# One LSTM step of a fused transformer kernel: both zero products side by side, the copies of the input part last on ScalarE, and the output rows reloaded step by step

## The chip, the cores and the metric

One Trainium2 chip, one core. The engines are named as the profile names them: PE (TensorE's matmuls), PEld (TensorE's weight loads), DVE (VectorE), ACT (ScalarE), POOL (GpSimd) and SP (SyncE, which issues most DMAs). The metric is device time in microseconds (us); lower is better.

## The reference, cut to what matters

A tokenizer with attention, a windowed attention layer, a mixture of experts, a phase-memory attention, and last an LSTM over T = 569 positions of 16 sequences, with D = 256 hidden units. All is fp32. What the change touches is the LSTM:

```python
x_proj = jnp.einsum('btd,gd->btg', x, W_ih) + b_ih + b_hh
def step(carry, xp):
    h, c = carry
    gates = xp + h @ W_hh.T
    i, f, g, o = jnp.split(gates, 4, axis=-1)
    c = jax.nn.sigmoid(f) * c + jax.nn.sigmoid(i) * jnp.tanh(g)
    h = jax.nn.sigmoid(o) * jnp.tanh(c)
    return ((h, c), h)
_, hs = jax.lax.scan(step, (h0, c0), jnp.swapaxes(x_proj, 0, 1))
```

After the scan, each position's output row adds a running sum over the positions before it and one over those behind it; the second needs the last position, so every output row gets one more addition at the end.

## The kernel before

Up to about 1710 us the kernel computes the tokenizer, the windowed attention and the experts. From there to about 3340 us it runs the 569 steps of the LSTM (the generator `steps()`, "the chain"), and between their instructions, up to step 505 or so, the phase-memory attention and the input products x @ W_ih of later blocks of positions ("the filler": `fronts`, `backs`). Up to the end it also runs the output sums of groups of finished steps (`all_sums`). The last 30 us add the last sum to all rows and store them.

The order on PE, DVE, ACT and POOL is fixed before the kernel runs: a planner (`class Order`) holds a table `STEP` with the cost of each part of a step, its engine and the part that it follows, and puts a piece of filler ahead of a part of the chain only where, by its own figures, it fits. SP's instructions are ordered by the compiler's tile framework. The framework also sets semaphore waits: an instruction that must wait for one semaphore carries the wait itself, and one that must wait for two gets an instruction EVENT_SEMAPHORE ahead of it on its engine, which carries the first.

One step, with the lines of the profile:

1. "hidden" (L1734): 16 matmuls of the hidden state X with W_hh, added to the PSUM tile GC (`gates`, 128x96: the gates i, f and g). "out hidden" (L1743): 8 matmuls into GO (`out_gate`, 128x64: gate o).
2. "gates" (L1754): ACT reads GC, tanh into `act`. "out gate" (L1760): ACT reads GO into `to`.
3. "clear" (L1684): four small bf16 matmuls with zeros, which set GC to zero and start its accumulation; "input" (L1691): ACT copies the next step's input part from `xc` into GC. The next "hidden" adds to it.
4. DVE: "products" `ab` (L1766), "cell" (L1772), "cell turned" `cT` (L1779).
5. "out clear" (L1684) of GO. From the last block but one on, eight spare matmuls with the identity matrix (L1085, `out_gate<-W_hh,ident`) stand ahead of it; they write to GO what the clear then overwrites.
6. "tangent" (L1787): ACT, tanh of the cell into `th`. Then "out input" (L1696): ACT copies `xo` into GO.
7. DVE: "out gate turned" (L1792), "state" X (L1794). X is what the next "hidden" waits for.

Each unit of 8 steps has its input part loaded by SP (one DMA `xc`, L1675, and four `xo`, L1679). Rows that are finished while filler runs are stored to a DRAM tile PD, since there is no room for them in SBUF. When the filler ends its SBUF is released, a tile O for all output rows takes its place, and SP reloads PD into O with eight DMAs of up to 1 MB (L1905). Later rows are written to O directly (L1863).

Of the kernel before, what the change touches and what calls it, by code (L numbers as in the profile page):

```python
# [10 lines left out]
F32 = mybir.dt.float32  # L11
BF16 = mybir.dt.bfloat16
AF = mybir.ActivationFunctionType
# [4 lines left out]
D = 256  # L18
# [67 lines left out]
def time_of_rows():  # L86
# [43 lines left out]
    "hidden": ("PE", 0.68, 0.85, "state", 0.055),  # L130
    "out hidden": ("PE", 0.24, 0.42, "hidden", -0.17),
    "gates": ("ACT", 0.16, 0.26, "hidden", 0.065),
    "clear": ("PE", 0.06, 0.25, "gates", 0.06),
    "out gate": ("ACT", 0.12, 0.22, "out hidden", 0.065),
    "input": ("ACT", 0.14, 0.24, "clear", 0.065),
    "products": ("DVE+", 0.22, 0.22, "gates", 0.035),
    "cell": ("DVE+", 0.19, 0.19, "products", 0.035),
    "cell turned": ("DVE", 0.13, 0.21, "cell", 0.035),
    "out clear": ("PE", 0.06, 0.25, "out gate", 0.06),
    "tangent": ("ACT", 0.14, 0.23, "cell turned", 0.095),  # L140
    "out input": ("ACT", 0.12, 0.22, "out clear", 0.065),
    "out gate turned": ("DVE", 0.15, 0.23, "out gate", 0.035),
    "state": ("DVE+", 0.18, 0.18, "tangent", 0.035),
}
# [150 lines left out]
def kernel(ctx: ExitStack, tc: tile.TileContext, a: dict, out: bass.AP):  # L295
    nc = tc.nc
# [1367 lines left out]
    def steps():  # L1664

        act = ls.tile([128, 4 * 32], F32, name="act_init", tag="act", bufs=3)
        nc.vector.memset(act[:, 96:], 0.0)
        before, begun, loaded = None, set(), set()  # L1670

        def load(k):
            j, u, n = UNITS_ALL[k]
            loaded.add(k)
            nc.sync.dma_start(  # L1675
                XC[k % 2][:, :n, :], XCD[j][:, :, u : u + n, :].rearrange("a b t x -> (a b) t x")
            )
            for q in range(4):
                nc.sync.dma_start(XO[k % 2][32 * q + NB : 32 * q + 32, :n, :], XOD[j][q, :, u : u + n, :])  # L1679
            plan.mark(("loaded", k), 4.0)  # L1680

        def clear(g, n, last):
            for q in range(4):
                nc.tensor.matmul(  # L1684
                    g[32 * q : 32 * q + 32, :n], nil[:, :32], nil[:, :n], start=True, stop=last
                )

        def begin(k, t):
            begun.add((k, t))
            yield "input"  # L1690
            nc.scalar.copy(GC[:, :96], XC[k % 2][:, t, :])  # L1691

        def begin_out(k, t):
            begun.add((k, t, "out"))
            yield "out input"
            nc.scalar.copy(GO[:, :64], XO[k % 2][:, t, :])  # L1696

        def ready(k):

            n = 2 * UNITS_ALL[k][0]  # L1700
            return [("back", n + i, slot) for i in range(2) for slot in range(2)]

        for k, (j, u, n) in enumerate(UNITS_ALL):
            if k not in loaded:
                for event in ready(k):
                    yield "at", event
                load(k)
            yield "at", ("loaded", k)

            after = [("back", 2 * (j + 1) + i, slot) for i in range(2) for slot in range(2)]  # L1710
            done = sum(plan.past(e) for e in after) if j + 1 < len(BLOCKS) else 4
            ahead = plan.past(("back", 2 * j + 3, 0))
            plan.spare = 0.0 if ahead else 0.2 if done >= 4.0 * u / BLOCKS[j][1] - AHEAD else 0.45
            if (j, u) in run_of:
                r = run_of[j, u]
                if r >= 4:
                    yield "at", ("sums", r - 4)
                hidden[r] = XS_OF[r % 4][:, :, : RUNS[r][2], :]
            X = hidden[r][:, :, u - RUNS[r][1] :, :]
            for t in range(n):  # L1720
                at, last = f"{k}_{t}", (k, t) == (len(UNITS_ALL) - 1, n - 1)
                if before is None:
                    yield "hidden"
                    clear(GC, 96, True)
                    clear(GO, 64, True)
                if (k, t) not in begun:
                    yield from begin(k, t)
                    yield from begin_out(k, t)
                yield "hidden"
                for kk in range(2 if before is not None else 0):  # L1730
                    for half in range(2):
                        for q in range(4):
                            own = 512 * (q // 2) + 96 * (2 * (q % 2) + half)
                            nc.tensor.matmul(  # L1734
                                GC[32 * q : 32 * q + NB * (1 + half), :96],
                                before[:, kk, NB * (1 - half) :], Whh[:, kk, own : own + 96],
                                start=False, stop=(kk + half == 2),
                            )
                yield "out hidden"
                for kk in range(2 if before is not None else 0):  # L1740
                    for q in range(4):
                        own = 512 * (q // 2) + 384 + 64 * (q % 2)
                        nc.tensor.matmul(  # L1743
                            GO[32 * q : 32 * q + 32, :64], before[:, kk, :],
                            Whh[:, kk, own : own + 64], start=False, stop=(kk == 1),
                        )
                if (
                    k + 1 < len(UNITS_ALL) and k + 1 not in loaded
                    and all(plan.past(e) for e in ready(k + 1))
                ):  # L1750
                    load(k + 1)
                nxt = (k, t + 1) if t + 1 < n else (k + 1, 0)
                yield "gates"
                nc.scalar.activation(act[:, :96], GC[:, :96], AF.Tanh, scale=0.5)  # L1754
                if not last:
                    yield "clear"
                    clear(GC, 96, False)
                to = ls.tile([128, 64], F32, name=f"to{at}", tag="to", bufs=3)
                yield "out gate"
                nc.scalar.activation(to, GO[:, :64], AF.Tanh, scale=0.5)  # L1760
                ahead = nxt[0] in loaded and plan.past(("loaded", nxt[0]))
                if ahead:
                    yield from begin(*nxt)
                ab = ls.tile([128, 2, 32], F32, name=f"ab{at}", tag="ab", bufs=2)
                yield "products"
                nc.vector.scalar_tensor_tensor(  # L1766
                    ab, act[:, :64].rearrange("p (g x) -> p g x", g=2), 1.0,
                    act[:, 64:].rearrange("p (g x) -> p g x", g=2), ALU.add, ALU.mult,
                )
                act = ls.tile([128, 4 * 32], F32, name=f"act{at}", tag="act", bufs=3)  # L1770
                yield "cell"
                nc.vector.scalar_tensor_tensor(  # L1772
                    act[:, 96:], ab[:, 1, :], 0.5, ab[:, 0, :], ALU.mult, ALU.add
                )


                cT = ls.tile([128, 2 * NB], F32, name=f"cT{at}", tag="cT", bufs=2)
                yield "cell turned"
                nc.vector.transpose(cT, act[:, 96:])  # L1779
                if not last:  # L1780
                    yield "out clear"
                    if j >= len(BLOCKS) - 2:
                        product(GO[:, :D], ident, Whh[:, 0, :D], start=True, stop=True)
                    clear(GO, 64, False)
                th = ls.tile([128, 2, NB], F32, name=f"th{at}", tag="th", bufs=2)
                yield "tangent"
                nc.scalar.activation(th.rearrange("p k x -> p (k x)"), cT, AF.Tanh, scale=0.5)  # L1787
                if ahead:
                    yield from begin_out(*nxt)
                toT = ls.tile([128, 2, 2 * NB], F32, name=f"toT{at}", tag="toT", bufs=2)  # L1790
                yield "out gate turned"
                nc.vector.transpose(toT.rearrange("p k x -> p (k x)"), to)  # L1792
                yield "state"
                nc.vector.scalar_tensor_tensor(  # L1794
                    X[:, :, t, NB:], toT[:, :, NB:], 1.0, th, ALU.add, ALU.mult
                )
                before = X[:, :, t, :]
            if u + n == RUNS[r][1] + RUNS[r][2]:
                plan.mark(("steps", r))

# [85 lines left out]
    with tc.manual_schedule(engines=ENGINES):  # L1886
# [13 lines left out]
        bg.close()  # L1900
        op = ctx.enter_context(tc.tile_pool(name="out", bufs=1))
        tail["O"] = op.tile([128, sum(map(len, UNITS_OF)), D], F32, name="O")
        for u in range(0, tail["stored"], 8):
            u1 = min(u + 8, tail["stored"])
            nc.sync.dma_start(tail["O"][:, u:u1, :], PD[:, u:u1, :])  # L1905
        plan.run([chain, rest])
    route.release()


# [153 lines left out]
```

## Time and profile before

| | |
|---|---|
| median of 3 runs | 3372.89 us (3368.87 to 3373.28) |
| the profiled execution | 3372.32 us, of which the span of its instructions is 3370.5 us |
| PE / DVE / ACT / POOL busy | 91% / 60% / 44% / 23% of the span |
| step 33 to step 481 (448 steps) | 1863.7 to 3092.0 us, 2.74 us per step |
| steps 514 to 569, without filler | 3192.7 to 3328.4 us, nearly all 2.50 us |
| end of the last step to the end | 3330 to 3370.5 us |

The table of waits tells for each engine and line how long it waited for whom, how often and how long at most. The chain in order of time follows back from the last instruction what released each instruction; "issue" in it is time in which nothing that the profile shows was waited for, such as the way of a semaphore from one engine to the next. ACTq is ACT's sequencer: there it is the EVENT_SEMAPHORE ahead of an ACT instruction.

### The profile page before, as it was taken

How to read it: one execution, taken by the hardware profiler on the slowest of the kernel's cores; microseconds unless marked ns; L12 is line 12 of the kernel's file. 1: busy time of each engine (PE TensorE's matmuls, PEld its weight loads, DVE VectorE, ACT ScalarE, POOL GpSimd, SP SyncE). 2: the span in 40 equal slices, each digit the busy share in tenths (PEclk: the TensorE clock that was granted, in tenths of full speed). 3: DMA queues.
4: the chain of work that ended last, by engine and by line, in shares of the span. 5: the costliest groups of instructions: out<-in, count | busy, mean ns of one | idle time of the engine just before them, and what ended most of it. 6: DMA issues, size and time to landing. Idle time of an engine off the chain costs nothing.

```text
span 3370.5 us, 135926 instructions
## 1 busy us (share of the span) xinstructions
PE 3069.8 (91%) x57536; PEld 2227.7 (66%) x57536; DVE 2013.5 (60%) x6785; ACT 1482.6 (44%) x5032; POOL 789.8 (23%) x1524
## 2 busy tenths in 40 slices
PE   6999989999859999997899999999999999999884
PEld 3666666666648888886565666666766666666552
DVE  4677777766732222222565777777777777776555
ACT  3545544454412222221443555555555555554442
POOL 1243554445533323222311011011111000100000
PEclk8999999999979999998999999999999999999997
DMA  5111221111176666663333333333333333333413
GB/s 179 53 41 62 89 79 51 55 39 40 42 254 231 224 224 228 226 234 130 110 95 78 94 82 80 86 90 87 87 82 90 91 83 84 81 91 79 144 36 117
DMA packets 272628, 366.39 MB, mean 109 GB/s; under 512 B 144097, under 2 KB 219793, under 8 KB 258961
## 3 DMA queue, kind: packets, MB, share of 16 engines
q1 hardware_dynamic: 250368, 308.51, 30.9%
q0 software_dynamic: 14496, 39.75, 3.1%
q8 instruction: 451, 7.39, 0.9%
q10 hardware_dynamic: 7152, 9.43, 0.9%
q14 instruction: 161, 1.31, 0.1%
HBM read 239.07 MB, written 118.49 MB: 106 GB/s over the span
## 4 chain that ended last, share of the span: by engine, by line
PE 40%; DVE 5%; ACT 3%; DMA 2%; issue 2%; POOL 0%; SPq 0%; ACTq 0%; DVEq 0%
PE gates L1734 12%; PE xm_False L1085 7%; PE out_gate L1743 3%; PE po_False L1085 2%; PE ek L1085 2%; PE v L1085 2%; PE eq L1085 2%; PE z L1085 2%; PE r_False L1085 1%; PE ds_False L1085 1%; PE out_gate L1684 1%; ACT act L1754 1%; PE gates L1684 1%; PE fin L1085 1%; DVE ab L1766 1%
## 5 line engine op out<-in xcount | busy, mean ns | idle before, releaser
L1734 PE MATMUL gates<-W_hh,X 128*16 128x96 f32 (+1 forms) x18176 | 487.7, 247 | 48.2 <-DVE X L1794 41.5
L1734 PEld LDWEIGHTS gates<-W_hh,X 128*16 128x16 f32 (+1 forms) x18176 | 377.5, 103 | 225.1 <-DVE X L1794 194.7
L1754 ACT ACTIVATE act<-gates 128x96 f32<-128x96 f32 x568 | 141.7, 249 | 462.9 <-PE gates L1734 453.8
L1248 ACT ACTIVATE hT<-hp,w 128x256 f32<-128x256 f32 x316 | 132.3, 471 | 481.2 <-PE hp L1241 314.1
L1766 DVE SCALAR_TENSOR_TENSOR ab<-act 128x64 f32<-128x64 f32 x568 | 127.8, 225 | 301.4 <-ACT act L1754 294.8
L1085 PE MATMUL xm_False<-W_ih,dxT_False 128*32 128x256 f32 x4352 | 294.3, 382 | 3.0 <-DVE xp_False L1591 1.2
L1255 PE MATMUL y<-w,hT 128*128 128x256 f32 x1264 | 289.7, 382 | 5.2 <-ACT hT L1248 1.5
L1241 PE MATMUL hp<-xt,w 128*128 128x256 f32 x1264 | 287.9, 381 | 1.0 <-ACT hT L1248 1.0
L1684 PEld LDWEIGHTS <-nil 128*32 128x32 bf16 x4552 | 176.4, 94 | 148.9 <-issue 55.9
L1255 PEld LDWEIGHTS y<-w,hT 128*128 128x128 f32 x1264 | 236.9, 190 | 45.1 <-ACT hT L1248 14.4
L1241 PEld LDWEIGHTS hp<-xt,w 128*128 128x128 f32 x1264 | 240.3, 191 | 35.7 <-ACT hT L1248 1.4
L1184 POOL DMA_INDIRECT YT<-ys,to x158 | 153.3, 970 | 439.9 <-DVE ys L1261 408.3
L1261 DVE TENSOR_TENSOR ys<-y,w 128x512 f32<-128x512 f32 x79 | 54.6, 691 | 316.6 <-PE y L1255 229.8
L1743 PE MATMUL out_gate<-W_hh,X 128*32 128x64 f32 x9088 | 233.8, 219 | 4.1 <-ACT out_gate L1696 2.6
L1691 ACT COPY gates<-xc 128x96 f32<-128x96 f32 x569 | 138.4, 243 | 176.9 <-PE gates L1684 104.9
L1743 PEld LDWEIGHTS out_gate<-W_hh,X 128*32 128x32 f32 x9088 | 186.9, 110 | 7.7 <-ACT out_gate L1696 2.9
L693 PE MATMUL wqk<-wxT,wqkv 128*128 128x128 f32 x1152 | 152.9, 281 | 8.6 <-ACT wxT L687 8.4
L908 POOL DMA_INDIRECT XS<-XN,at x144 | 148.9, 1034 | 45.6 <-issue 24.6
L693 PEld LDWEIGHTS wqk<-wxT,wqkv 128*128 128x128 f32 x1152 | 141.7, 194 | 25.3 <-ACT wxT L687 13.4
L1794 DVE SCALAR_TENSOR_TENSOR X<-toT,th 128x32 f32<-128x32 f32 x569 | 107.5, 189 | 77.7 <-ACT th L1787 72.4
L1298 POOL TENSOR_SCALAR r_False_rstd<-r_False_mv,cols 128x2 f32<-128x2 f32 x36 | 15.7, 436 | 584.4 <-DVE r_False_mv L1293 584.3
L1684 PE MATMUL gates<-nil 128*32 128x96 bf16 x2276 | 131.1, 209 | 23.7 <-ACT act L1754 18.5
(356 smaller groups left out, 6509.7 us busy)
## 6 DMA issues: line engine op xcount, KB each, us to landing
w<-in_wpack SPq DMA_DIRECT2D x79, 1154.0 KB
taps<-in_taps SPq DMA_DIRECT2D x16, 1764.0 KB
xc<-XCD SPq DMA_DIRECT2D x71, 384.0 KB
XCD<-xp_False SPq DMA_DIRECT2D x256, 96.0 KB
xs<-XS SPq DMA_DIRECT2D x79, 258.0 KB
yg<-YT SPq DMA_DIRECT2D x72, 256.0 KB
HD<-h SPq DMA_DIRECT2D x72, 128.0 KB
fh<-HD SPq DMA_DIRECT2D x72, 128.0 KB
```

What stands on the lines that cost most here:

```text
L693: nc.tensor.matmul(qk[:, j, m, :], wqkv[:, k, D * j + 128 * m : D * j + 128 * m + 128], xT[:, k, :], start=(k == 0), stop=(k == 1),)
L908: fill(0, nc.gpsimd.indirect_dma_start(out=XS[0], out_offset=bass.IndirectOffsetOnAxis(ap=at[:, i, c - lo : c - lo + 1], axis=0), in_=XN[p ...
L1085: nc.tensor.matmul(out[own], lhsT[:, own], rhs, start=start, stop=stop)
L1184: keep(nc.gpsimd.indirect_dma_start(out=YT, out_offset=bass.IndirectOffsetOnAxis(ap=to[:, i : i + 1], axis=0), in_=ys[:, i, :], in_offset= ...
L1241: nc.tensor.matmul(hp[:, i, :], w1[:, k, hc * 128 : (hc + 1) * 128], xT[:, k, :], start=(k == 0), stop=(k == 1),)
L1255: nc.tensor.matmul(y[:, i, :], hT[:, hc, 128 * i : 128 * i + 128], w2[:, hc, :], start=(hc == 0), stop=(hc == 3),)
L1684: nc.tensor.matmul(g[32 * q : 32 * q + 32, :n], nil[:, :32], nil[:, :n], start=True, stop=last)
L1691: nc.scalar.copy(GC[:, :96], XC[k % 2][:, t, :])
L1734: nc.tensor.matmul(GC[32 * q : 32 * q + NB * (1 + half), :96], before[:, kk, NB * (1 - half) :], Whh[:, kk, own : own + 96], start=False, ...
L1743: nc.tensor.matmul(GO[32 * q : 32 * q + 32, :64], before[:, kk, :], Whh[:, kk, own : own + 64], start=False, stop=(kk == 1),)
L1754: nc.scalar.activation(act[:, :96], GC[:, :96], AF.Tanh, scale=0.5)
L1766: nc.vector.scalar_tensor_tensor(ab, act[:, :64].rearrange("p (g x) -> p g x", g=2), 1.0, act[:, 64:].rearrange("p (g x) -> p g x", g=2), ...
```

## The change

- The two clears of a step stand side by side, after "out gate", with the spare matmuls ahead of both.
- "input" and "out input" come last in the step on ACT, after "tangent" (in the code, `begin` now holds both copies).
- The framework is told that ACT's reads of GC and GO (L1754, L1760) and ACT's copies into them need no semaphore between each other, because a PE product stands between them.
- The planner's table `STEP` gets the new order and new costs.
- PD is reloaded by pieces of two rows, one DMA per step at the end of the step, issued on ACT.

Cut to its core:

```diff
-    "clear": ("PE", 0.06, 0.25, "gates", 0.06),
     "out gate": ("ACT", 0.12, 0.22, "out hidden", 0.065),
-    "input": ("ACT", 0.14, 0.24, "clear", 0.065),
+    "clear": ("PE", 0.11, 0.3, "out gate", 0.06),
...
-    "out clear": ("PE", 0.06, 0.25, "out gate", 0.06),
-    "tangent": ("ACT", 0.14, 0.23, "cell turned", 0.095),
-    "out input": ("ACT", 0.12, 0.22, "out clear", 0.065),
+    "tangent": ("ACT", 0.18, 0.23, "cell turned", 0.04),
+    "input": ("ACT", 0.18, 0.24, "clear", 0.065),
+    "out input": ("ACT", 0.16, 0.22, "clear", 0.065),
...
+            begun[k, t] = nc.scalar.copy(GC[:, :96], XC[k % 2][:, t, :])
+            ordered_by_products(begun[k, t], read.pop(0, None))
             yield "out input"
-            nc.scalar.copy(GO[:, :64], XO[k % 2][:, t, :])
+            begun[k, t, 1] = nc.scalar.copy(GO[:, :64], XO[k % 2][:, t, :])
+            ordered_by_products(begun[k, t, 1], read.pop(1, None))
+
+        def ordered_by_products(ins, other):
+            if other is not None and before is not None:
+                tc.declare_no_dep(
+                    ins.ins, other.ins, reason="a product between them waits for the first"
+                )
+            return ins
...
                 yield "gates"
-                nc.scalar.activation(act[:, :96], GC[:, :96], AF.Tanh, scale=0.5)
+                read[0] = ordered_by_products(
+                    nc.scalar.activation(act[:, :96], GC[:, :96], AF.Tanh, scale=0.5), begun.pop((k, t))
+                )
+                to = ls.tile([128, 64], F32, name=f"to{at}", tag="to", bufs=3)
+                yield "out gate"
+                read[1] = ordered_by_products(
+                    nc.scalar.activation(to, GO[:, :64], AF.Tanh, scale=0.5), begun.pop((k, t, 1))
+                )
                 if not last:
                     yield "clear"
+                    if j >= len(BLOCKS) - 2:
+                        product(GO[:, :D], ident, Whh[:, 0, :D], start=True, stop=True)
                     clear(GC, 96, False)
-                to = ls.tile([128, 64], F32, name=f"to{at}", tag="to", bufs=3)
-                yield "out gate"
-                nc.scalar.activation(to, GO[:, :64], AF.Tanh, scale=0.5)
-                ahead = nxt[0] in loaded and plan.past(("loaded", nxt[0]))
-                if ahead:
-                    yield from begin(*nxt)
+                    clear(GO, 64, False)
...
                 yield "cell turned"
                 nc.vector.transpose(cT, act[:, 96:])
-                if not last:
-                    yield "out clear"
-                    if j >= len(BLOCKS) - 2:
-                        product(GO[:, :D], ident, Whh[:, 0, :D], start=True, stop=True)
-                    clear(GO, 64, False)
                 th = ls.tile([128, 2, NB], F32, name=f"th{at}", tag="th", bufs=2)
                 yield "tangent"
                 nc.scalar.activation(th.rearrange("p k x -> p (k x)"), cT, AF.Tanh, scale=0.5)
-                if ahead:
-                    yield from begin_out(*nxt)
+                if nxt[0] in loaded and plan.past(("loaded", nxt[0])):
+                    yield from begin(*nxt)
...
                 before = X[:, :, t, :]
+                if tail.get("reload"):
+                    part = tail["reload"].pop(0)
+                    nc.scalar.dma_start(tail["O"][:, part, :], PD[:, part, :])
...
-        for u in range(0, tail["stored"], 8):
-            u1 = min(u + 8, tail["stored"])
-            nc.sync.dma_start(tail["O"][:, u:u1, :], PD[:, u:u1, :])
+        tail["reload"] = [slice(u, min(u + 2, tail["stored"])) for u in range(0, tail["stored"], 2)]
         plan.run([chain, rest])
```

More of the change, by code (lines that the diff above doesn't have):

```diff
@@ L1669, in steps @@
         nc.vector.memset(act[:, 96:], 0.0)
-        before, begun, loaded = None, set(), set()
+        before, begun, loaded, read = None, {}, set(), {}
         def load(k):
@@ L1688, in begin @@
         def begin(k, t):
-            begun.add((k, t))
             yield "input"
-            nc.scalar.copy(GC[:, :96], XC[k % 2][:, t, :])
-        def begin_out(k, t):
-            begun.add((k, t, "out"))
+            begun[k, t] = nc.scalar.copy(GC[:, :96], XC[k % 2][:, t, :])
+            ordered_by_products(begun[k, t], read.pop(0, None))
             yield "out input"
-            nc.scalar.copy(GO[:, :64], XO[k % 2][:, t, :])
+            begun[k, t, 1] = nc.scalar.copy(GO[:, :64], XO[k % 2][:, t, :])
[6 more added lines that the diff above has]
+            return ins
         def ready(k):
@@ L1727, in steps @@
                     yield from begin(k, t)
-                    yield from begin_out(k, t)
                 yield "hidden"
@@ L1902 @@
         tail["O"] = op.tile([128, sum(map(len, UNITS_OF)), D], F32, name="O")
-        for u in range(0, tail["stored"], 8):
-            u1 = min(u + 8, tail["stored"])
-            nc.sync.dma_start(tail["O"][:, u:u1, :], PD[:, u:u1, :])
+        tail["reload"] = [slice(u, min(u + 2, tail["stored"])) for u in range(0, tail["stored"], 2)]
         plan.run([chain, rest])
+        assert not tail["reload"]
     route.release()
```

## The prediction

> **What bounds the kernel now.** First the table of stretches: busy time of PE, PEld, DVE, ACT and POOL, then the granted clock, DMA share and GB/s.
>
> ```profile
> 2600.00:2800.00 200.00, 193.96 (x5938) 136.73 (x5942) 150.39 (x575) 111.44 (x444) 19.26 (x48) 1.00 0.36 91
> 3188.00:3338.00 150.00, 117.08 (x3688) 78.84 (x3680) 79.08 (x341) 64.26 (x285) 0.00 (x0) 0.98 0.09 24
> ```
>
> With filler PE is 97% busy, without it 78%. But a busy PE does not say who is late. The table of waits does:
>
> ```profile
> PEld gates L1734 <- DVE X L1794: 194.7, 428, 1.0
> ```
>
> In 428 of 568 steps the first weight load of "hidden" finds nothing ahead of it and waits for X, 0.45 us on average. PE's matmuls are still draining then, so PE looks busy, but the step's length is set by the chain X, hidden, gates, cell, tangent, X. A microsecond on that chain counts 428 times, with filler or without. One step of it, from the chain in order of time:
>
> ```profile
> 3240.61 0.02 issue
> 3240.63 0.02 ACTq L1754
> 3240.65 0.04 issue
> 3240.69 0.26 ACT act L1754
> ...
> 3241.68 0.02 issue
> 3241.70 0.24 ACT th L1787
> 3241.94 0.02 issue
> 3241.97 0.20 DVE X L1794
> 3242.17 0.04 issue
> 3242.21 0.90 PE gates L1734 x32
> ```
>
> Each hop costs 0.02 to 0.04 us, save the one from PE to `act`, 0.08 us: there an EVENT_SEMAPHORE (ACTq) takes the first of two waits. The copies into PSUM and PE's work ahead of them are in the timeline (start, length):
>
> ```profile
> 3241.19 0.64 PE L1085 MATMUL out_gate<-W_hh,ident 128*32 128x256 f32 x8
> 3241.32 0.24 ACT L1691 COPY gates<-xc 128x96 f32<-128x96 f32 x1 [0.18 <-PE gates L1684]
> 3241.99 0.22 ACT L1696 COPY out_gate<-xo 128x64 f32<-128x64 f32 x1
> ```
>
> Both end well ahead of "hidden" or beside it: no row of the chain is a copy.
>
> **The change part by part.** The program's order shows where the waits go. ACT's EVENT_SEMAPHOREs fall from 2671 to 1038, but PE's rise from 371 to 927. `act`, `to` and the copies now wait for PE alone. But ACT had learnt from those waits how far its own work was, and PE had learnt from X that the copy into GC was done, since X came behind `th` and `th` behind the copy. Both lose that: `th` now waits for DVE and ACT (565 of 569 steps), the first matmul of "hidden" for DVE and ACT (560 of 568), with DVE's wait in the EVENT_SEMAPHORE ahead of them. So two double waits come onto the chain and one leaves it.
>
> `act`: 0.08 us becomes 0.02: −0.06 us a step.
>
> `th`: the nearest row with both waits is the exponential in the tokenizer, which waits for DVE and ACT:
>
> ```profile
> 853.39 0.62 DVE L585 TENSOR_REDUCE ttop<-tsc 128x1 f32<-128x441 f32 x1 [0.86 <-PE tsc L579]
> 854.11 0.63 ACT L589 ACTIVATE tP<-tsc,ttop 128x441 f32<-128x441 f32 x1 [1.82 <-DVE ttop L585]
> ```
>
> The reduction ends at 854.01, the exponential starts 0.10 us later; `th` starts 0.03 us behind `cT` now. That is +0.06 to +0.07, so `act` and `th` cancel.
>
> "hidden": nearest is a matmul of the filler that waits for DVE and PE, with DVE last:
>
> ```profile
> 2740.79 0.44 DVE kT L1271
> 2741.23 0.14 issue
> 2741.36 0.64 PE r_False L1085 x8
> ```
>
> 0.14 us where "hidden" has 0.04: +0.10. Its weight load stands 0.03 us ahead of it (2741.33), so counted by weight loads it is +0.06. I take 0.085: the matmul is what "hidden" ends by. Ends 0.06 and 0.10.
>
> The copy as the later of the two: it can start when `th` leaves ACT; `to` starts 0.02 us before `act` ends, so from 3241.91, and ends at 3242.15, X at 3242.16. The clear of GC now stands behind the spare matmuls, where the clear of GO ended at 3241.86 and its copy started 0.13 us later; by that the copy ends at 3242.23. With 0.05 us to PE it is ready by 3242.20 to 3242.28; X with its double wait lets "hidden" start at 3242.30. So X stays last, by 0.02 to 0.10 us.
>
> Sum for the chain: 428 x 0.085 = +36 us (26 to 43). In the other 140 steps the wait lies under PE's queue, and I cost it at nothing; if it showed there too it would be 12 more.
>
> The planner's order: the same 493,792 columns of filler end in the same step, but less evenly. Between steps 33 and 480, steps with fewer than 512 columns rise from 13 to 29, and those with 1152 or more from 48 to 58. A piece of 256 columns takes 0.43 us (1.31 us for three, `xm_False` L1085 in the chain). Sixteen more light steps that leave one piece open are 7 us, two pieces 14; nothing if the heavy steps have room. I take +10 (0 to 15). The clears cost nothing more: they are the same instructions, under PE's queue.
>
> The reload: the chain of waits shows it where the filler ends.
>
> ```profile
> 3161.95 10.97 DMA O<-PD
> 3172.94 12.46 DMA xo<-XOD
> ```
>
> SP issued eight reloads between the first and the second of a unit's four `xo` loads, and the next input part came late. But the chain went on beside it: `act` of step 505 starts at 3158.99, of step 514 at 3190.24; nine steps took 31.25 us against 9 x 2.50 and 0.3 for the sums in them. So the whole stall is 8.4 us, not 23. Cut into 30 pieces of 256 KB behind no `xo`, I take all of it: −8.4. Nearest rows for issuing on ACT: DMAs there take ACT's sequencer 0.41 us in the experts, up to 1.57 us in the last stores; ACT has 0.8 us between "out input" and `act`. At 0.41 it is hidden; at the upper end it would be 30 x 0.75 = 22 us, which I count to a quarter in the range (+5).
>
> A rule speaks against the part of this that rests on another queue. The Trainium skill ("DMA: Bandwidth & Descriptors", "Issuing engines are not separate DMA queues") says that DMAs issued by different engines run on the same 16 DMA engines and interleave, and that a second issuer saves only issue time. By it the gain would be the cutting's alone, at worst nothing, and the sum 8.4 us higher.
>
> What comes new at that place: the first write to O must wait until the last stores out of the released SBUF have landed. Before, the last addition ended at 3156.64 and the write to O (L1863) started at 3161.01, 4.4 us later, two steps on, off the path. In the new order this write stands on DVE directly behind the last addition and ahead of the next `ab`. The addition ends 0.7 us after X, so `ab` gets DVE at 0.7 + 4.4 + 0.8 (two writes) = 5.9 us after X instead of 1.3: +4.5 us once (0 to 4.5). The first reload on ACT waits for the same landing, beside it.
>
> Against the profiled execution's own 3372.3 us (its median stands 0.6 above that): 3372.3 + 36 + 10 − 8.4 + 4.5 = 3414.4.
>
> **The rivals.** *Faster*: a second wait that is already met might cost nothing, on `th` and on "hidden"; then only `act`'s −0.06 stays: −0.06 x 428 = −26, with the reload −8, about 3338. It decides if the rise of `th` behind `cT` and of "hidden" behind X stays under 0.02 us each. Against it: `r_False`'s other wait was long met and still 0.14 us passed.
>
> *No change*: PE is 97% busy, so the filler may take up the chain's delay; then only the 56 steps from 3188 us on pay, 56 x 0.085 = 5, which with −8.4 and +4.5 gives 3373. Against it: 428 waits of 0.45 us.
>
> *Copy last*: if filler ahead of the clears, or ACT's work, lets the copy end over 0.09 us after X, the copy sets "hidden". 0.1 us more in the 428 steps is +43: about 3457. For it: the margin is 0.02 to 0.10 us, and the clears now lie behind all filler that came between the two before.
>
> **How the numbers follow.** Forecast 0.75, copy last 0.12, faster 0.08, no change 0.05. Low end: 26 + 0 − 8.4 + 0 = +18, 3390. High end: 43 + 15 + 0 (the rule) + 4.5 + 5 = +67, 3440; what is left out is the copy last, the faster case and the even one. One measurement tells about 0.2% (6.7 us) from no change. Faster by more 0.07, within 0.05, slower 0.88.
>
> **What would show it.** In the chain after: `th` about 0.09 us behind `cT`, "hidden" 0.11 to 0.14 behind X, an ACTq row no longer ahead of `act` but ahead of `th`, a PEq row or a longer issue ahead of "hidden", and steps of 2.58 us instead of 2.50 where no filler is. No DMA row of over 3 us near the filler's end, and one step of some 7 us there. I am wrong if steps without filler stay at 2.50 us or fall, if the copies L1691 and L1696 come into the chain, or if waits for X become rarer with filler.

## The result, and the profile after

The changed kernel takes 3475.6 us (median of 4 runs, 3469.4 to 3480.2) against 3372.3: 1.0311 times as long (95% interval 1.0298 to 1.0324), +103 us. The direction was right, the size was not: +42 was forecast, and the time lies 36 us above the range. The profiled execution took 3469.4 us, its span 3467.6 us.

One step behind the filler, from the chain of waits of the kernel after (start, length, what):

```profile
3301.81 0.22 DVE cT L1786
3302.03 0.02 issue
3302.05 0.02 ACTq L1789
3302.07 0.04 issue
3302.11 0.23 ACT th L1789
3302.34 0.18 ACT gates L1689
3302.52 0.15 ACTq L1802
3302.67 0.00 ACT out_gate L1692
3302.68 0.21 issue
3302.89 0.89 PE gates L1737 x32
3303.77 0.02 issue
3303.80 0.26 ACT act L1758
```

As the prediction had it, the ACTq row has left `act` and stands ahead of `th`, and "hidden" starts late: 560 of its 568 steps have an EVENT_SEMAPHORE of 0.05 us ahead of the first weight load (PEldq is the sequencer of PE), which the kernel before has nowhere at this line:

```profile
L1737 PEldq EVENT_SEMAPHORE  x560: 51/51/51, 1715.0 to 3422.9; - x187
```

But the chain runs over the two copies (L1689, L1692) and not over X. The table of waits says the same (engine, line, what it waited for: us in all, times, longest):

```profile
ACT th L1789 <- DVE cT L1786: 284.7, 479, 5.0
PEld gates L1737 <- ACT out_gate L1692: 251.9, 462, 4.9
ACT gates L1689 <- DMA xc<-XCD: 68.0, 7, 17.1
```

The prediction had said that copies in the chain would prove it wrong. Whether "hidden" really waits for a copy has to be decided by experiment, because `out_gate` L1692 is a name that the profile infers from which event came last, and by the program "hidden" does not wait for that copy at all (its matmuls write GC, not GO). The timeline has the four candidates, start and length:

```profile
3302.28 0.24 ACT L1689 COPY gates<-xc 128x96 f32<-128x96 f32 x1
3302.38 0.19 DVE L1796 SCALAR_TENSOR_TENSOR X<-toT,th 128x32 f32<-128x32 f32 x1 [0.23 <-ACT th L1789]
3302.46 0.21 ACT L1692 COPY out_gate<-xo 128x64 f32<-128x64 f32 x1
3302.68 0.51 PEld L1737 LDWEIGHTS gates<-W_hh,X 128*16 128x16 f32 x16 [0.57 <-ACT out_gate L1692]
```

The copy into GC ends at 3302.52, X at 3302.57, the copy into GO at 3302.67, the first weight load follows at 3302.68. Beside filler the copy into GC is seldom last either: of the 441 steps from 33 to 480 that do not end a block of 64, it ends after X in 20, and what it ends later than 0.06 us after X comes to 3.5 us in all.

Two other rows matter. PE stands still where the profile shows nothing to wait for, here in the middle of "out hidden" (8 matmuls in the program, 16 rows in the profile; chain of the kernel after):

```profile
2452.59 0.19 PE out_gate L1746 x10
2452.78 1.45 issue
2454.24 0.26 PE out_gate L1746 x3
```

And the seven waits for the input part of the next block have grown. In the kernel before they read:

```profile
ACT gates L1691 <- DMA xc<-XCD: 55.0, 7, 13.0
```

Laid out by stretches (from one `act` to the next, both traces): steps 33 to 480, where filler lies between the steps, take 1228.3 us before and 1316.0 after. Seven of these steps stand at the end of a block of 64 (steps 96, 160 and so on to 480); the chain there waits until the filler has made the next block's input. They took 70.0 us together and take 105.7: +36. The other 441 steps took 1158.3 and take 1210.3: +52. The first 32 steps are 6 us longer, the last 54 5 us longer, steps 481 to 514, where the reload was, 2.4 us shorter.

The granted clock, the share of its full clock that PE had by the profile, differs a little too. Between steps 33 and 480 PE ran at half its clock for 3.4 us in the trace before and for 27.3 us in the trace after, in six pieces; PE had been busy for at most 2.5 of the 4 us ahead of each. If every microsecond at half the clock costs half of one, that is 12 us more than before (an estimate, and an upper one); no run separates it from the rest of the 88 us.

### The profile page after: what moved, and what is told of

It is laid out like the page before. It is cut to its first block, busy times and chain, and to the rows that moved or that the text cites. A ratio compares the mean times of both kernels' runs of the same rounds, so it can differ in the third digit from the quotient of the medians.

```text
span 3467.6 us, 134874 instructions
## 1 busy us (share of the span) xinstructions
PE 3066.9 (88%) x57536; PEld 2272.3 (66%) x57536; DVE 2039.6 (59%) x6809; ACT 1430.0 (41%) x5008; POOL 785.8 (23%) x1524
## 4 chain that ended last, share of the span: by engine, by line
PE 29%; DVE 9%; ACT 9%; issue 4%; DMA 2%; SPq 1%; POOL 0%; ACTq 0%; DVEq 0%
PE gates L1737 12%; PE xm_False L1084 4%; ACT act L1758 2%; ACT th L1789 2%; DVE ab L1773 2%; DVE cT L1786 2%; DVE act L1779 2%; PE out_gate L1746 2%; PE ek L1084 1%; ACT gates L1689 1%; ACT out_gate L1692 1%; PE eq L1084 1%; PE po_False L1084 1%; PE v L1084 1%; PE z L1084 1%
## 5 line engine op out<-in xcount | busy, mean ns | idle before, releaser
L1737 PE MATMUL gates<-W_hh,X 128*16 128x96 f32 (+1 forms) x18176 | 501.0, 249 | 118.1 <-ACT out_gate L1692 89.3
L1737 PEld LDWEIGHTS gates<-W_hh,X 128*16 128x16 f32 (+1 forms) x18176 | 398.3, 103 | 282.9 <-ACT out_gate L1692 251.9
L1746 PE MATMUL out_gate<-W_hh,X 128*32 128x64 f32 x9088 | 254.0, 221 | 12.4 <-issue 10.9
L1789 ACT ACTIVATE th<-cT 128x32 f32<-128x32 f32 x569 | 130.3, 229 | 288.2 <-DVE cT L1786 284.7
L1746 PEld LDWEIGHTS out_gate<-W_hh,X 128*32 128x32 f32 x9088 | 202.3, 111 | 18.4 <-issue 16.0
L1689 ACT COPY gates<-xc 128x96 f32<-128x96 f32 x569 | 133.9, 235 | 88.0 <-DMA xc<-XCD 68.0
L1084 PEld LDWEIGHTS xm_False<-W_ih,dxT_False 128*32 128x32 f32 x4352 | 128.3, 110 | 51.4 <-DVE xp_False L1590 7.4
```

The source lines that it names most:

```text
L1084: nc.tensor.matmul(out[own], lhsT[:, own], rhs, start=start, stop=stop)
L1689: begun[k, t] = nc.scalar.copy(GC[:, :96], XC[k % 2][:, t, :])
L1737: nc.tensor.matmul(GC[32 * q : 32 * q + NB * (1 + half), :96], before[:, kk, NB * (1 - half) :], Whh[:, kk, own : own + 96], start=False, ...
L1746: nc.tensor.matmul(GO[32 * q : 32 * q + 32, :64], before[:, kk, :], Whh[:, kk, own : own + 64], start=False, stop=(kk == 1),)
```

## The experiments

**The theories.** A: "hidden" now has two waits; the second costs 0.09 us a step on the chain and leaves PE short of instructions. O: the rest is the order in which the planner lays the filler. The rivals: it is the zero products standing together (B); second waits cost nothing (C); the reload only moves its stall (D); the copies, which the table of waits names, set the start of "hidden" (E); the gaps of PE follow the chain's length (F); PE is so full of filler that a shorter chain gains nothing (P).

Where the experiments ran, the kernel before takes 3380 to 3386 us instead of 3372, so ratios to it are compared; the kernel after was not run again there, and where a distance to it is given in us it is the difference of the two ratios. One row for each; "gaps" are stretches over 0.3 us between steps 33 and 480 in which PE neither multiplies nor loads weights and waits for nothing that the trace shows; the last two columns are the seven block-boundary steps and the 441 others, in us. Steps and distances (end of X to the first matmul of "hidden", end of `cT` to `th`) are medians over the last 52 steps, where no filler is.

| kernel | ratio to before (95%) | step | X to hidden | cT to th | gaps: us | boundaries | others |
|---|---|---|---|---|---|---|---|
| before | 1 | 2.500 | 0.054 | 0.034 | 7: 4.5 | 70.0 | 1158.3 |
| after | 1.0311 (1.0298 to 1.0324) | 2.586 | 0.145 | 0.094 | 23: 18.3 | 105.7 | 1210.3 |
| e1 copy behind tangent | 1.0239 (1.0208 to 1.0270) | 2.584 | 0.145 | 0.034 | 23: 22.5 | 75.8 | 1228.3 |
| e2 no self-waits | 0.9982 (0.9966 to 0.9998) | 2.501 | 0.054 | 0.094 | 6: 4.1 | 65.1 | 1153.9 |
| e3 rows by steps | 0.9988 (0.9975 to 1.0000) | 2.500 | 0.054 | 0.034 | 4: 3.9 | 68.2 | 1163.7 |
| e4 zero product ahead | 1.0152 (1.0116 to 1.0187) | 2.501 | 0.054 | 0.093 | 8: 4.3 | 108.6 | 1176.0 |
| e5 one planner number | 1.0076 (1.0059 to 1.0093) | 2.500 | 0.056 | 0.034 | 7: 5.6 | 99.8 | 1157.9 |
| e6 zero products together | 1.0141 (1.0124 to 1.0158) | 2.956 | 0.056 | 0.492 | 7: 3.6 | 76.0 | 1175.3 |
| e7 planner told | 1.0135 (1.0118 to 1.0152) | 2.586 | 0.146 | 0.094 | 24: 20.2 | 36.7 | 1237.7 |
| e8 kept parts, other order | 0.9928 (0.9912 to 0.9945) | 2.500 | 0.054 | 0.095 | 7: 3.9 | 48.4 | 1171.0 |
| e9 both causes removed | 1.0041 (1.0027 to 1.0055) | 2.500 | 0.054 | 0.095 | 7: 5.8 | 69.1 | 1170.4 |
| e10 tangent freed | 0.9878 (0.9862 to 0.9895) | 2.445 | 0.055 | 0.034 | 6: 2.5 | 47.1 | 1158.5 |
| e11 hidden alone with two | 1.0260 (1.0243 to 1.0277) | 2.527 | 0.146 | 0.034 | 29: 21.4 | 105.5 | 1198.7 |

**e1: the copy into GC behind the tangent, alone.**

```diff
-                if ahead:
-                    yield from begin(*nxt)          # ahead of "products"
...
                 if ahead:
+                    yield from begin(*nxt)          # behind "tangent"
                     yield from begin_out(*nxt)
```

> The kernel before with one edit: the copy of the input part into GC stands behind the tangent on ACT instead of ahead of the products; zero products, waits of ACT on itself and reload as before. So only the first matmul of 'hidden' gets a second wait (DVE in an EVENT_SEMAPHORE, then ACT, in 561 of 568 steps); 'act' and 'th' keep their waits.
> Theory A (the second wait of 'hidden' is the cost on the chain, and its EVENT_SEMAPHORE also leaves PE short of instructions): steps without filler rise by 0.09 to 0.10 us to 2.59-2.60, gaps of PE over 0.3 us that nothing explains rise from 7 to 15 or more between steps 32 and 480, the sum of the steps that are no block boundary rises by 40 to 60 us; total 3410 to 3435.
> Rival B (the zero products together are the cost, through the order in which filler is laid): 3370 to 3385, steps of 2.50 us.
> The seven steps at block boundaries depend on the order that the planner makes of it; 60 to 90 us together.

Measured: 1.0239, 3464.7 us, above the 3410 to 3435 of theory A. This edit alone costs some 80 us. The distance to "hidden" rises by 0.091 us and nothing else in the chain moves, so a step is 2.584 us; the gaps of PE triple. The other steps rise by 70 us, of which 441 x 0.084 = 37 are the chain's and 18 the gaps'; some 15 were not taken apart (the filler lies in another order here, and PE ran at half its clock for 17.1 us instead of 3.4). Against the 40 to 60 us expected for these steps that is too much as well.

**e2: no waits of ACT on itself, alone.** The declarations of the change between copies and reads are put into the kernel before, and nothing else.

> The kernel before with one edit: the declarations that take ACT's waits on itself away between copies and reads. 'act' waits for PE alone, 'th' gets DVE and ACT; 'hidden' keeps its one wait, and the order of the filler stays the same to the instruction.
> Theory A: -0.06 us on 'act' and +0.07 on 'th' cancel: steps without filler 2.50 to 2.52 us, boundaries 70 us as before, unexplained gaps of PE as few as before; total 3365 to 3380.
> Rival C (a second wait that is met costs nothing on ACT): steps of 2.44 us, total 3340 to 3350.

Measured: 0.9982. In its chain `act` follows "hidden" without ACTq, and `th` has it instead:

```profile
3287.33 0.22 DVE cT L1790
3287.55 0.02 issue
3287.57 0.02 ACTq L1798
3287.59 0.04 issue
3287.63 0.24 ACT th L1798
```

The step stays at 2.50 us: what `act` gains `th` loses, as forecast. "Hidden" keeps its one wait. So its second wait in the kernel after does not come from ACT's missing waits on itself but, with e1, from the copy's place.

**e3: output rows by steps, alone.** The reload of the change in the kernel before.

> The kernel before with one edit: the output rows are reloaded two units at a time behind the steps, from ACT.
> Theory A (the reload's stall of 8.4 us goes, the write to O costs up to 4.5 us once): steps 504 to 514 fall from 33.7 to about 30 us with one step of some 7 us among them; all before that as it was; total 3363 to 3369.
> Rival D (the reload only moves its stall to other steps or to the end): 3370 to 3377.

Measured: 0.9988, -4.1 us (interval -8.5 to 0). Steps 505 to 514 fall from 33.7 to 26.4 us; one step of 4.9 us, not of 7, stands at the filler's end. The total fits theory A at its small end but does not separate it from D, nor from no change; the steps do. The small stall of 4.9 us is step 504, just ahead of the ten.

**e4: the kernel after with one zero product of one column ahead of "hidden".**

```diff
                 yield "hidden"
+                if before is not None:
+                    nc.tensor.matmul(GC[:32, :1], nil[:, :32], nil[:, :1], start=False, stop=False)
```

> The kernel after with one addition: ahead of 'hidden' stands one zero product of one column into GC. It takes the wait for the copy into GC (ACT), so that the first matmul of 'hidden' waits for DVE alone and PE's EVENT_SEMAPHOREs fall from 926 to 366; the order of the filler, the copies and all else stay the same to the instruction.
> Theory A: 'hidden' stands 0.04 to 0.05 us behind X instead of 0.11, steps without filler fall by 0.06 to 0.09 us to 2.50-2.52, unexplained gaps of PE fall from 23 back to under 12, and the boundaries stay at 100 to 108 us, since the order is the same; total 3415 to 3440.
> Rival E (the copies, now last on ACT, set the start of 'hidden', as the table of waits names them): nothing gained, 3470 to 3480.
> Rival B (order alone): 3465 to 3480.

Measured: 1.0152, 3438.6 us; 1.6% or 54 us (give or take 13) below the kernel after. From its timeline (the zero product is PE L1734):

```profile
3280.20 0.24 ACT L1689 COPY gates<-xc 128x96 f32<-128x96 f32 x1
3280.30 0.19 DVE L1798 SCALAR_TENSOR_TENSOR X<-toT,th 128x32 f32<-128x32 f32 x1 [0.23 <-ACT th L1791]
3280.38 0.21 ACT L1692 COPY out_gate<-xo 128x64 f32<-128x64 f32 x1
3280.50 0.16 PE L1734 MATMUL gates<-nil 128*32 128x1 bf16 x1 [0.32 <-ACT gates L1689]
3280.55 0.45 PEld L1739 LDWEIGHTS gates<-W_hh,X 128*16 128x16 f32 x22 [0.48 <-DVE X L1798]
```

The copies stand to X as in the kernel after, to within 0.01 us: the copy into GC ends at 3280.44, X at 3280.49, the copy into GO at 3280.59. But "hidden" starts at 3280.55, before the copy into GO ends. The copies did not set its start; rival E falls, and with it the name in the table of waits. What cost 0.09 us was that one instruction had two waits and the late one, X, stood in the EVENT_SEMAPHORE. The zero product takes the early wait, and X is the only one left. The gaps of PE fall back to 8 with it. The table of waits, PE alone, first of this kernel and then of the kernel after:

```profile
PE out_gate L1748 <- issue: 2.2, 4, 0.7
```

```profile
PE out_gate L1746 <- issue: 10.9, 16, 1.9
```

The boundaries stay at 108.6 us, as the unchanged order of the filler asks.

e4 also measures the order of the kernel after. It has that order with the step and the gaps of the kernel before, and still takes 1.52% or 51 us longer than it; in its trace 39 us of that are boundaries. The reload's gain (e3) and the added matmuls are in this figure, and so is a clock that stood at half for 47.8 us in this trace, that of the slowest of its four runs.

**e5: the kernel before with one number of the planner changed.**

```diff
-    "hidden": ("PE", 0.68, 0.85, "state", 0.055),
+    "hidden": ("PE", 0.68, 0.85, "state", 0.085),
```

> The kernel before with one number of the planner's table changed: it counts 0.085 us instead of 0.055 from X to 'hidden'. No instruction is added, removed or given another wait for its own sake; only the order in which filler is laid between the steps changes.
> Theory O (the sums of the block-boundary steps come from where the planner lays the filler): the seven boundaries rise from 65-70 us to 90-110, as in the kernel after; steps without filler stay at 2.50, unexplained gaps of PE under 10; the other steps fall by up to 15 us, since the filler is spread thinner there; total 10 to 30 us above before (3395 to 3415).
> Rival (the boundaries rose in the kernel after because its chain was slower): boundaries 65 to 72, total 3378 to 3392.

Measured: 1.0076, +26 us, with the chain at 2.50 us and no more gaps than before. The boundaries rise from 70 to 99.8 us by the order of filler alone; theory O. That the other steps fall by up to 15 us was not seen (1157.9).

**e6: both zero products together, alone**, behind "out gate" in the kernel before, with the copies where they were.

> The kernel before with one edit: both zero products stand together behind 'out gate', as in the kernel after; the copies stay where they were (GC ahead of the tangent, GO behind it), waits and reload too.
> Theory A: the zero product of GC now lies behind the spare product and behind filler, so the copy into GC ends later, and the tangent stands behind that copy on ACT. At the end, where the spare product takes 0.64 us of PE, steps rise from 2.50 to 2.8-3.0 us (54 steps: +16 to +27 us); between steps 32 and 480 by 0.02 to 0.06 us each. 'hidden' keeps its one wait. Total 3415 to 3450. Then the copies had to be put behind the tangent for the zero products to stand together.
> Rival (the same instructions in another place cost nothing): 3380 to 3395.

Measured: 1.0141. Its chain at the end:

```profile
3291.26 0.23 ACT to L1756
3291.49 0.04 issue
3291.53 0.64 PE out_gate L1084 x8
3292.17 0.04 PE gates L1683 x4
3292.21 0.09 PE out_gate L1683 x4
3292.31 0.02 issue
3292.33 0.07 ACT gates L1690
3292.40 0.10 issue
3292.50 0.23 ACT th L1784
```

DVE's row `cT` is gone from the chain: the tangent waits on ACT behind the copy, the copy for the zero products, these for the spare product of 0.64 us, and that for `to`. Steps become 2.96 us. So with the spare product ahead of both zero products, as the change has it, the copies have to go behind the tangent, and that costs the second wait on "hidden" (e1). The zero product of GC ahead of the spare product was not tried.

**e7: the kernel after, its planner told of the two waits.**

```diff
-    "hidden": ("PE", 0.68, 0.85, "state", 0.055),
+    "hidden": ("PE", 0.68, 0.85, "state", 0.14),
...
-    "tangent": ("ACT", 0.18, 0.23, "cell turned", 0.04),
+    "tangent": ("ACT", 0.18, 0.23, "cell turned", 0.1),
```

> The kernel after with two numbers of the planner's table changed to what its profile shows: 0.14 us from X to 'hidden' (0.055), 0.10 from the turned cell to the tangent (0.04). Every instruction keeps its waits; only the order of the filler changes.
> Theory O: the boundaries fall from 106 us to 35-70, part of it comes back in the other steps (+10 to +25), the steps without filler stay at 2.585 and the unexplained gaps of PE at 15 to 25; total 3430 to 3460.
> Rival (boundaries follow the slower chain): boundaries 100 to 110, total 3468 to 3485.

Measured: 1.0135, 1.8% or 59 us below the kernel after, by the order of filler alone: the step is still 2.586 us, the gaps are 24. The boundaries fall to 36.7 us; the waits for the input part say so too:

```profile
ACT gates L1689 <- DMA xc<-XCD: 26.0, 4, 15.9
```

27 us of the 69 come back in the other steps, a little more than the 10 to 25 expected. The total is a little under the 3430 to 3460 expected.

**e8: what is worth keeping.** The kernel before with the edits of e2 and e3, and the planner's number from X to "hidden" at 0.145.

> The kernel before with two parts of the change (ACT's waits on itself away; output rows reloaded by steps) and the planner's number from X to 'hidden' at 0.145 us. Zero products and copies as before, so 'hidden' has one wait.
> Theory A with O: steps without filler 2.50, stall of the reload gone (-5 to -7 us between steps 504 and 514), -6 for the self-waits as measured alone, boundaries 45 to 60 us instead of 65 to 70, other steps up by 0 to 8; total 3355 to 3378, below the kernel before.
> Rival (the planner's number was best where it was): boundaries 70 or more, total 3375 to 3400.

Measured: 0.9928, 3356.3 us, as theory A with O had it; the boundaries fall to 48.4 us, but the other steps rise by 13 us where 0 to 8 was expected.

**e9: the kernel after with the zero product of e4 and that number at 0.145.**

> The kernel after with the zero product of one column ahead of 'hidden' (so that 'hidden' waits for DVE alone) and the planner's number from X to 'hidden' at 0.145 us instead of 0.055 (so that filler is laid in another order). Nothing else is changed.
> Theory A with O (the two waits of 'hidden' and the filler's order are the whole of the loss): steps without filler 2.50, unexplained gaps of PE under 10, boundaries 60 to 75 us, no stall of the reload; total 3365 to 3395, within 0.5% of the kernel before.
> Rival (a third cause costs 20 us or more): above 3400.

Measured: 1.0041, 3391.3 us: 2.70 of the 3.11% are gone, which is 91 of 105 us here. Taken singly the two edits of e4 and e7 were worth 54 and 59, 22 more than that. But e9 has not the table of e7 (which also changes the tangent's number), so its order is another, with boundaries of 69.1 us instead of 36.7; whether the two causes overlap no run tells. What is left, 0.4%, was not taken apart; the first 32 steps (156.4 us against 148.6) hold about half of it.

**e10: `th` freed as well.** In the kernel of e8 the copy into GC keeps its wait for `act`:

```diff
             begun[k, t] = nc.scalar.copy(GC[:, :96], XC[k % 2][:, t, :])
-            ordered_by_products(begun[k, t], read.pop(0, None))
```

> The kernel of two kept parts in another order of filler (step behind the tangent and 'hidden' as before), with one more edit: the copy into GC keeps its wait for 'act' on ACT, 0.6 us ahead of X and off the chain. ACT learns by it how far its own work is, so 'th' waits for DVE alone while 'act' still waits for PE alone.
> Theory A: 'th' stands 0.03 us behind 'cT' instead of 0.09, steps without filler fall to 2.44 us, the steps at the end by 3 us in all, those that wait for X between steps 32 and 480 by 0.06 each where PE is not full; total 10 to 26 us below the 3356 of that kernel: 3330 to 3347.
> Rival P (PE full of filler takes it up): 3350 to 3362.

Measured: 0.9878, 3340.6 us: 40 us below the kernel before and the fastest version. No ACTq is left in its chain:

```profile
3182.47 0.26 ACT act L1761
3182.73 0.02 issue
...
3183.24 0.22 DVE cT L1789
3183.47 0.02 issue
3183.49 0.24 ACT th L1797
3183.73 0.02 issue
3183.75 0.20 DVE X L1804
3183.95 0.04 issue
3184.00 0.90 PE gates L1740 x32
```

**e11: the kernel after with the edit of e10**, so that "hidden" alone has two waits.

> The kernel after with one edit: the copy into GC keeps its wait for 'act' on ACT. So 'act' and 'th' have one wait each, 'hidden' keeps two, and the order of the filler stays the same to the instruction.
> Theory A (the gaps of PE follow the EVENT_SEMAPHORE ahead of 'hidden'): steps without filler 2.52 to 2.53, unexplained gaps still 18 to 28, boundaries 100 to 110; total 15 to 27 us below the kernel after, 2.3 to 2.8% above before.
> Rival F (the gaps follow the longer chain): with the step a third as far above 2.50 as in the kernel after, gaps of about 12 or fewer, and a total under 2.2% above before.

Measured: 1.0260, 17 us below the kernel after. The step falls to 2.527 us, the gaps do not fall with it (29). They follow the EVENT_SEMAPHORE ahead of "hidden", not the length of the chain: 23 to 29 in the four kernels that have it, 4 to 8 in the nine that have not. Where no filler is, another thing sets the step here. With `th` earlier, X ends 0.07 us ahead of the copy into GC, which waits for the zero products and the spare product, and the chain runs over that copy:

```profile
3291.09 0.25 ACT gates L1689
3291.35 0.07 issue
3291.41 0.89 PE gates L1736 x32
```

"Hidden" starts as far behind X as in the kernel after (0.146), and its weight load 0.05 behind the copy, so the two waits end together here. Between steps 33 and 480 X is the last in most steps (by 0.085 us, median), as in the kernel after.

## Why the prediction was wrong

In short, two terms of the sum failed: the planner's order, taken at +10 us, was worth some 51, and the second wait of "hidden", taken at +36, some 54.

**The bound.** Right: X, "hidden", gates, cell, tangent set the step; e4 and e10 take 0.085 and 0.055 us off it against the kernel that they alter, and gain 1.6 and 0.5%, although most steps lie beside filler.

**The chain's terms.** Right in size. `th` +0.060 (0.06 to 0.07 said), "hidden" +0.091 for the matmul and +0.062 for its weight load (0.085 taken), from the first matmul of "hidden" to `act` -0.07 (-0.06), the step +0.086 (0.085). The copy ends 0.05 us ahead of X (0.02 to 0.10 said), so the rival "copy last" did not happen, though the time lies near its 3457 and beyond, and though the profile's names spoke for it: e4 shows it without filler, and beside filler the late copies add up to 3.5 us.

**What the chain's term lacked.** 428 x 0.085 = 36 stood for the whole cost of the second wait. e4 takes that wait away in an unchanged order and gains 54 us (41 to 67). The surplus has its clearest part in the gaps of PE: 18.3 us against 4.5 in the trace. No step of the prediction asked what else an EVENT_SEMAPHORE on PE holds up. Of the other 140 steps, costed at nothing, some paid as well: in the kernel after the weight load of "hidden" waits 462 times instead of 428, for 252 us instead of 195.

**The planner's order.** This is the step that failed most: +10 us, 0 to 15, where e4 leaves 51 us (39 to 63) for the order and the smaller parts together. The seven boundaries alone are 36 us longer, e5 shows that order alone moves them by 30 without any instruction changed, and e7 takes 59 us off the kernel after by order alone. The prediction counted how many steps get few or many columns of filler. That misses where the pieces stand on which the next block's input hangs: where these come late in a block, the chain waits at its end in one go. The row with the seven waits for XC, 55 us in all, was in the table of waits of the kernel before; it should have been the basis of this term, and its range: e4, e5, e7 and the kernel after lie between 37 and 109 us.

**The reload.** The stall went, no DMA of over 3 us is left in the chain near the filler's end, and e3 measures -7.3 us in those steps (-8.4 said), -4.1 in all. Whether the other queue or the cutting brought it no run separates, so the rule of the Trainium skill ("DMA: Bandwidth & Descriptors", "Issuing engines are not separate DMA queues"), that another issuer saves only issue time, is neither shown nor refuted here. The issue on ACT took 0.33 us (0.41 taken), beside other work. The write to O made one step of 7.57 us in the kernel after, 5.0 above the others (+4.5 said), and of 4.9 in e3, 2.4 above.

**The rivals.** "Faster" and "no change" fell as argued: a second wait costs 0.06 us on ACT and 0.09 on PE (e2, e1), and the filler did not take it up (e4 gains more than the chain's share).

## What to carry to other kernels

Where a planner lays filler around a chain, a changed step table is a change of its own: price it at the places where the chain waits for the filler (here seven, 37 to 109 us in all), give it both signs, and separate it on the chip by a version that changes the table and nothing else. Before moving an instruction behind the one by which another engine learnt of it, count the waits of the first instruction that needs both; if it gets two, let a small instruction ahead of it take the one that is met first. And where only the name that the profile gives to a wait speaks for a cause, change the form of the wait and leave the named instruction where it is.

## What the runs showed of the hardware

A second wait is not free, even where it is met before the other; in the rows measured here the later of the two stands in the EVENT_SEMAPHORE: 0.060 us on ACT (e2), 0.091 on PE (0.062 to its weight load; e1 and the kernel after). With the early one taken by an instruction of its own in front, the price is nothing that can be seen (0.054 us from X to "hidden" in e4 as in the kernel before), although that adds a matmul to every step.

PE may run out of instructions. The trace has a queue that goes with PE's instructions: 453 packets of 16 KB for the 116,002 of the kernel after, 451 for the 115,446 of the kernel before, 455 for the 116,578 of e4, about 256 instructions to a packet each time. In the kernel after:

```profile
q8 instruction: 453, 7.42, 0.9%
```

Of the 23 gaps there between steps 33 and 480, 22 end 2.3 to 2.9 us after the start of such a packet (the other 3.5, behind a packet that took 2.1 instead of about 1.0 us); the packets start 4.65 us apart on average, 283 of them in 1316 us, so this is no accident. In e1, e7 and e11 75 of the 76 gaps end 2.2 to 3.1 us after such a start. The Trainium skill says on "Runtime: NRT & Kernel Launch" ("Instruction fetch mechanics") that instructions are fetched in blocks of 16 KiB while the current ones run, at a cost that is mostly hidden. The size agrees, and in the nine kernels with a single wait on "hidden" only 4 to 8 gaps of this kind show; with the EVENT_SEMAPHORE there, if the fetch is what PE waits for, it is hidden less: 18 to 23 us in these stretches. "Perfetto Trace Analysis" ("Per-engine timelines") describes a matmul's wait as one in a queue, during which the sequencer decodes on, and that of a sequencer-only instruction as one that the sequencer itself sits out. If the EVENT_SEMAPHORE is of the second kind, that would explain why PE has no stock of decoded instructions when a new block is due; no run here shows it. The runs show that the gaps come and go with the EVENT_SEMAPHORE; that the fetch is what PE waits for rests on the coincidence in time and was not tried by itself.
